# Cross-attention tile stage: whole-array products replaced by 32-row products, four tiles at a time

## The chip, the cores and the metric

The kernel runs on one core of one Trainium2 chip. The metric is the device time of one execution in microseconds (us). A profiled execution also has a span, the time from its first to its last recorded instruction, and the rows of the profile are read against that span.

## The reference

The reference is one layer of cross-attention in fp32. A text `x` of shape (4, 2048, 512) attends to a context of shape (4, 77, 384).

```python
text_p  = x @ W_text + b_text                      # 512 -> 512
audio_p = ctx @ W_audio + b_audio                  # 384 -> 512
Q = layer_norm(text_p, g1, beta1)
K = layer_norm(audio_p, g2, beta2);  V = audio_p
alpha = softmax(Q @ K.T / sqrt(512))               # over 77 keys
H = (alpha @ V) @ W_out + b_out
return layer_norm(H + x, g_out, beta_out)
```

Both kernels rearrange this. `W_text` is centred over its output channels, so that the mean of the layer norm falls away. The scores of a row are then `x` times a matrix M (512 x 77, one for each batch element), scaled by the row's reciprocal standard deviation. The variance of a row is the quadratic form x G x with G = W W^T, plus a linear term (one more column of M) and a constant. As G is symmetric, a triangle of it is enough: blocks off the diagonal are doubled, blocks above it are left out. V and `W_out` are multiplied once for each batch element, so that a row's output is its 77 softmax weights times a 77 x 512 matrix, plus `x`, normalized.

## The kernel before

The rows of `x` are worked on in 64 tiles of 128 rows; four tiles are a group, four groups a batch element. For each tile TensorE needs `x` turned (channels on partitions). That is done by VectorE's 32 x 32 block transpose, `turn` (L403), on a copy of `x` that the DMA has spread so that the blocks land in place (`spread_x`, L177, runs of 512 bytes); a second copy in natural order, `load_x` (L165), serves the residual and the quadratic form.

The tile stage, tile by tile:

- `project_chunks` multiplies the turned tile by `mu`, which holds M and the triangle of G side by side. It takes four chunks of 128 channels, each against 464, 464, 336 and 208 columns (L452), into one PSUM bank `y`, and the last 128 x 128 block of G into a second bank `yl` (L460).
- `score` (L498, L476) adds the score offsets and sums y times x, which gives the row's variance; `score_last` (L476) does the same for `yl`.
- `row_scale` (L506, L212) makes the reciprocal standard deviation on GpSimd; `scale_scores` (L513, L516), `exponential` (L523) and `invert` (L549) make the softmax weights, four tiles at a time.
- `turn_weights` transposes the weights on TensorE (L535) and copies them out on ScalarE (L536); `apply` multiplies them by the 77 x 512 matrix (L543).
- `residual` (L556) adds `x`, `squares` (L564) sums the squares, `deviations` (L576, L212) makes the reciprocal deviation. Three of four tiles are normalized on ScalarE (`norm_on_scalar`, L609) and GpSimd (`norm_on_gpsimd`, L613 and L614), the fourth by two VectorE passes (`norm_on_vector`, L593 and L595). `store` (L583) sends 128 rows to DRAM.

Ahead of the tile stage stands a preparation of some 37 us: keys and values (L246 to L309), the turned `W_text` (L634), G in `gram` (L645) and `gram_out` (L658 to L660), M in `score_weights` (L340 to L351). `value_weights` (L382) runs on TensorE between the first three tiles.

Each engine executes its instructions in the order in which the program issues them (`in_program_order`). That order is written out: a loop over the first 40 tiles and then a list of letters and tile numbers, `p` for the first half of `project_chunks`, `P` for its second half, `a` for `apply`, and so on. All DMAs are issued from the queue of SyncE (SP). PSUM has eight banks: two `y`, two `yl`, two `h`, and two for other things; `bank` hands them out. The last tiles go through softmax in twos and then one by one (`LAST`).

Of the kernel before, what the change touches and what calls it, by code (L numbers as in the profile page):

```python
# [48 lines left out]
def tile_xattn(  # L49
# [30 lines left out]
    xio = ctx.enter_context(tc.tile_pool(name="xio", bufs=5))  # L80
    xqs = ctx.enter_context(tc.tile_pool(name="xqs", bufs=2))
    scrap = ctx.enter_context(tc.tile_pool(name="scrap", bufs=1))
    soft = ctx.enter_context(tc.tile_pool(name="soft", bufs=4))
    work = ctx.enter_context(tc.tile_pool(name="work", bufs=3))
    zs = ctx.enter_context(tc.tile_pool(name="zs", bufs=13))
    small = ctx.enter_context(tc.tile_pool(name="small", bufs=8))
    ps1 = ctx.enter_context(tc.tile_pool(name="ps1", bufs=1, space=bass.MemoryType.PSUM))
    ps2 = ctx.enter_context(tc.tile_pool(name="ps2", bufs=2, space=bass.MemoryType.PSUM))

    def bank(tag, name):  # L90
        return (ps2 if tag in ("h", "y") else ps1).tile([P, 4, P], F32, tag=tag, name=name)

# [11 lines left out]
    SQ = -(-(S + 1) // Q)  # L104
    S1 = Q * SQ
    LAST_K = ND - 1
    AQ = SQ + LAST_K * R
    assert Q == ND and Q * AQ <= 4 * P

# [19 lines left out]
    wa = const.tile([P, NA, H], F32, name="wa")  # L129
# [12 lines left out]
    wc = xqs.tile([P, ND, T, P], F32, tag="xq", name="wc").rearrange("p k t c -> p k (t c)")  # L142
# [13 lines left out]
    rows = load("rows", [P, H], b_text.partition_broadcast(P))  # L156

    groups = [(b, g) for b in range(B) for g in range(NG)]
    xs, xq = {}, {}

    def load_x(i):
        if i < len(groups):
            b, g = groups[i]
            t = xio.tile([P, T, D], F32, tag="x", name=f"x_{i}")
            nc.sync.dma_start(  # L165
                out=t,
                in_=x[b, g * T * P : (g + 1) * T * P, :].rearrange("(t p) d -> p t d", p=P),
            )
            xs[i] = t

    def spread_x(i):
        if i < len(groups):
            b, g = groups[i]
            t = xqs.tile([P, T, Q, P], F32, tag="xq", name=f"xq_{i}")
            rows = x[b, g * T * P : (g + 1) * T * P, :].rearrange("(a j) c -> j a c", j=R)
            for q in range(Q):
                nc.sync.dma_start(  # L177
                    out=t[q * R : (q + 1) * R].rearrange("j t a c -> j (t a) c"),
                    in_=rows[:, :, q * P : (q + 1) * P],
                )  # L180
            xq[i] = t

    spread_x(0)
    wo = load("wo", [P, NH, H], w_out.rearrange("(k p) h -> p k h", p=P))
    bo = load("bo", [P, H], b_out.partition_broadcast(P))
    load_x(0)
    load_x(1)
    go = load("go", [P, H], g_out.partition_broadcast(P))
    beo = load("beo", [P, H], beta_out.partition_broadcast(P))
    spread_x(1)  # L190
# [23 lines left out]
    wct = const.tile([P, NH, D], F32, name="wct")  # L214
# [6 lines left out]
    mu = [const.tile([P, ND, Q, AQ], F32, name=f"mu_{i}") for i in range(2)]  # L221
    ub = const.tile([P, Q, R], F32, name="ub")

    def parts(t):
        return t.rearrange("p (q m) -> p q m", q=Q)

    made = {}
# [3 lines left out]
    va, kn, mvs, krs, vws = {}, {}, {}, {}, {}  # L231
    sizes = [z - a for a, z in key_blocks]
    columns = [slice(a, z) for a, z in key_blocks]
    cat = prep.tile([P, NA, N], F32, name="cat")
    vat = prep.tile([P, NH, N], F32, name="vat")
    kt = prep.tile([P, NH, N], F32, name="kt")
    kg = prep.tile([P, NH, B, S1], F32, name="kg")
    later = prep.tile([P, ND, B - 2, S1], F32, name="later")
# [33 lines left out]
    def values_out(j, pv):  # L272
        ba = bav[:, j : j + 1]
        if j % 2:
            nc.scalar.activation(vat[:, j], pv, AF.Identity, bias=ba)
        else:
            nc.vector.tensor_scalar(vat[:, j], pv, ba, None, ALU.add)
# [18 lines left out]

    def normed(i):

        n = sizes[i]
        kn[i] = prep.tile([P, H], F32, name=f"kn_{i}")[:n]  # L300
        nc.vector.tensor_scalar(
            kn[i], va[i], mvs[i][:n, 0:1], krs[i][:n], ALU.subtract, ALU.mult
        )
# [28 lines left out]
    def score_bank(k, tag):  # L332
        pms[k] = flat(bank(tag, f"m_ps_{k}"))[:, : B * S1].rearrange("p (b s) -> p b s", s=S1)
        nc.vector.memset(pms[k][:, :, S + 1 :], 0.0)

    def score_weights(k):

        pm = pms[k]
        for j in range(NH):
            nc.tensor.matmul(  # L340
                pm[:, :, : S + 1],
                lhsT=wct[:, j, k * P : (k + 1) * P],
                rhs=kg[:, j, :, : S + 1],
                start=(j == 0),
                stop=(j == NH - 1),
            )
        for b in range(2):
            (nc.vector.tensor_copy if b else nc.scalar.copy)(
                mu[b][:, k, :, :SQ], parts(pm[:, b, :])
            )  # L350
        nc.scalar.copy(later[:, k], pm[:, 2:, :])  # L351

    def score_offsets():
# [7 lines left out]
        for v in range(2):  # L361
            for h in range(2):
                (nc.vector.tensor_copy if h else nc.scalar.copy)(
                    uws[h * HP : (h + 1) * HP, :, v, :S],
                    pu[v * HP : (v + 1) * HP].rearrange("p (b s) -> p b s", s=S),
                )
        nc.vector.memset(uws[:, :, 0, S:], 0.0)
        nc.vector.tensor_scalar_add(bc2, bc2, H * EPS)

    vw = [  # L370
        batch.tile([P if b < 2 else S, H], F32, name=f"vw_{b}") for b in range(B)
    ]
    for b in range(B):
        made[b] = mu[b % 2], uws[:, b], vw[b][:S]

    def value_weights():

        for i, n in enumerate(sizes):
            vws[i] = (vw[i] if i < 2 else prep.tile([P, H], F32, name=f"vws_{i}"))[:n]
            pv = flat(bank("prep", f"vw_ps_{i}"))[:n]  # L380
            for j in range(NH):
                nc.tensor.matmul(  # L382
                    pv, lhsT=vat[:, j, columns[i]], rhs=wo[:, j, :], start=(j == 0), stop=(j == NH - 1)
                )
            yield
            nc.vector.tensor_tensor(vws[i], pv, bo[:n], ALU.add)
        for b in range(2, B):
            for i, (r0, r1) in enumerate(key_blocks):
                a, z = max(b * S, r0), min((b + 1) * S, r1)
                if a < z:  # L390
                    nc.sync.dma_start(
                        out=vw[b][a - b * S : z - b * S], in_=vws[i][a - r0 : z - r0]
                    )

    NT = len(groups) * T
    turned = {}

    def turn(n):

        i, t = divmod(n, T)  # L400
        if n < NT:
            xt = work.tile([P, ND, P], F32, name=f"xt_{n}", tag="xt")
            nc.vector.transpose(  # L403
                xt.rearrange("p k (a j) -> p a k j", j=R),
                xq[i][:, t].rearrange("p a (k i) -> p a k i", i=R),
            )
            turned[n] = xt


    LAST = [2, 2, 2, 2, 2, 2, 2, 1, 1]  # L410
    batches, start = [], 0
    for size in [T] * ((NT - sum(LAST)) // T) + LAST:
        batches.append(range(start, start + size))
        start += size
    batch_of = {n: tiles for tiles in batches for n in tiles}

    ys, state, kept, scored_y, in_bank = {}, {}, [], [], {}
    begun = [-1]

    class Batch:  # L420


        def __init__(self, tiles):
            f, self.tiles, self.m = tiles[0], tiles, len(tiles)
            self.uw, self.vw = made[groups[f // T][0]][1:]
            self.w = kept[0][:, groups[f // T][0], :S] if kept else self.uw[:, 1, :S]
            self.e = soft.tile([P, T, S1], F32, name=f"e_{f}", tag="e")

            def columns(name):
                return small.tile([P, T], F32, name=f"{name}_{f}", tag=name)  # L430

            self.ss, self.rs = map(columns, ("ss", "rs"))
            self.mx, self.inv = map(columns, ("mx", "inv"))
            self.sz, self.sq, self.ro, self.nm = map(columns, ("sz", "sq", "ro", "nm"))
            self.z = {}

    def of(n):

        tiles = batch_of[n]
        f = tiles[0]  # L440
        if f not in state:
            state[f] = Batch(tiles)
        return state[f], slice(n - f, n - f + 1)


    def project_chunks(n, ks):
        mub = made[groups[n // T][0]][0]
        xt = turned[n]
        y, b = ys[n]
        for k in ks:  # L450
            cols = slice(0, SQ + min(k + 1, LAST_K) * R)
            nc.tensor.matmul(  # L452
                parts(y[:, : Q * AQ])[:, :, cols],
                lhsT=xt[:, k, :],
                rhs=mub[:, k, :, cols],
                start=(k == LAST_K),
                stop=(k == 0),
            )
            if k == LAST_K:
                nc.tensor.matmul(  # L460
# [429 lines left out]
```

## Time and profile before

| | |
|---|---|
| median of 3 runs | 293.08 us (293.02 to 293.49) |
| span of the profiled execution | 291.9 us |
| TensorE busy | 283.0 us (97%) |
| VectorE busy | 227.1 us (78%) |
| GpSimd busy | 157.2 us (54%) |
| ScalarE busy | 153.3 us (53%) |
| DMA packets | 54178, 55.33 MB |
| first tile product (L452) starts | 37.21 us |

The profile came without a device time of its own for the profiled execution; its span is 1.2 us under the median of the runs. A row of a group reads: line, engine, operation, output tile from input tiles, shape, count, then busy us and the mean ns of one, then the idle time of the engine ahead of it and what ended that idle time. A row of the timeline starts with the time in us from the start of the span and the length. The ends of matmuls are modelled, so their spacing is read from their starts.

### The profile page before, as it was taken

What the parts mean: (1) busy time and instruction counts of PE and PEld (TensorE: products, weight loads), DVE (VectorE), ACT (ScalarE), POOL (GpSimd) and SP (SyncE); (2) the same over time, 40 slices, a digit from 0 to 9 for tenths busy, and PEclk for the clock granted to TensorE, in tenths of its full rate; (3) what the DMA queues carried; (4) which work ended last, traced back from release to release, by engine and by line L of the source; (5) the groups of instructions that cost most, each with busy time, mean ns of one, the idle gap of its engine ahead of it and who ended that gap; (6) DMA issues with size and microseconds to landing.
All of it is one profiled execution on the core that took longest, in us unless ns stands there. A gap on an engine that the chain in (4) does not pass through costs nothing.

```text
span 291.9 us, 4021 instructions
## 1 busy us (share of the span) xinstructions
PE 283.0 (97%) x1034; PEld 171.6 (59%) x1034; DVE 227.1 (78%) x715; ACT 153.3 (53%) x486; POOL 157.2 (54%) x168
## 2 busy tenths in 40 slices
PE   8999999999999999999999999999999999999990
PEld 7786755565555555555555555556555556555540
DVE  1586133586878888888888989898999999989995
ACT  2646210031446383838383838366967767477571
POOL 1022000011026576757676767687989878977833
PEclk9999999999999999999999999999999999999996
DMA  6899913359390967887777878789689887612214
GB/s 200 212 267 370 214 65 99 61 183 249 92 227 36 186 245 161 274 171 263 167 265 165 269 162 270 160 274 206 262 174 294 200 270 204 159 72 88 108 58 180
DMA packets 54178, 55.33 MB, mean 190 GB/s; under 512 B 2597, under 2 KB 35697, under 8 KB 54155
## 3 DMA queue, kind: packets, MB, share of 16 engines
q1 hardware_dynamic: 54155, 55.07, 70.0%
q8 instruction: 8, 0.13, 0.2%
q14 instruction: 15, 0.12, 0.2%
HBM read 37.97 MB, written 16.78 MB: 188 GB/s over the span
## 4 chain that ended last, share of the span: by engine, by line
PE 94%; DVE 3%; issue 1%; DVEq 0%; ACT 0%
PE y L452 53%; PE h L543 18%; PE yl L460 5%; PE vw_ps L382 4%; PE m_ps L340 3%; PE vat_ps L264 3%; PE et_ps L535 2%; PE w_ps_yl L645 2%; PE w_ps_yl L208 1%; PE w_ps_y L645 1%; DVE z L595 1%; PE uw_ps L358 1%; DVE z L556 1%; DVE y L593 1%; PE va_ps L284 0%
## 5 line engine op out<-in xcount | busy, mean ns | idle before, releaser
L452 PE MATMUL y<-mu,xt 128*128 128x464 f32 (+2 forms) x512 | 179.6, 473 | 0.0
L452 PEld LDWEIGHTS y<-mu,xt 128*128 128x128 f32 x512 | 89.7, 190 | 49.6 <-issue 32.3
L543 PE MATMUL h<-vw,et 77*128 77x512 f32 x128 | 64.1, 594 | 0.1
L564 ACT ACTIVATE sqj<-z,sz 128x512 f32<-128x512 f32 x64 | 46.0, 718 | 31.9 <-DVE z L556 31.0
L613 POOL TENSOR_TENSOR z<-z,go 128x512 f32<-128x512 f32 x44 | 56.0, 1272 | 10.0 <-ACT z L609 9.4
L614 POOL TENSOR_TENSOR z<-z,beo 128x512 f32<-128x512 f32 x44 | 55.9, 1271 | 3.5
L556 DVE SCALAR_TENSOR_TENSOR z<-h,inv,x 128x512 f32<-128x512 f32 x64 | 46.5, 733 | 2.3 <-PE h L543 1.7
L403 DVE STREAM_TRANSPOSE xt<-xq 128x512 f32<-128x512 f32 x64 | 44.7, 704 | 0.5 <-PE y L452 0.5
L476 DVE CUSTOM_DVE_ANT_1 yl<-yl,x,bc 128x128 f32<-128x128 f32 x64 | 22.6, 353 | 28.2 <-PE yl L460 28.1
L476 DVE CUSTOM_DVE_ANT_1 y<-y,x,e 128x384 f32<-128x384 f32 x64 | 40.1, 626 | 2.3
L506 POOL TENSOR_SCALAR rs<-ss 128x4 f32<-128x4 f32 (+2 forms) x21 | 4.7, 223 | 66.9 <-DVE ss L476 66.6
L460 PEld LDWEIGHTS yl<-ub,xt 128*128 128x128 f32 x128 | 23.6, 188 | 26.2 <-issue 15.6
L609 ACT ACTIVATE z<-z,no,ro 128x512 f32<-128x512 f32 x44 | 34.5, 802 | 0.1
L536 ACT COPY et<-et_ps 77x256 f32<-77x256 f32 (+1 forms) x33 | 11.9, 361 | 39.5 <-PE et_ps L535 39.5
L212 POOL TENSOR_TENSOR ro<-ro,mhalf 128x4 f32<-128x4 f32 (+2 forms) x21 | 18.2, 867 | 23.7 <-ACT ro L576 23.6
L523 ACT ACTIVATE e<-e,mx 128x77 f32<-128x77 f32 x64 | 22.2, 349 | 11.9 <-DVE mx L516 11.9
L543 PEld LDWEIGHTS h<-vw,et 77*128 77x128 f32 x128 | 23.3, 190 | 7.0 <-issue 5.2
L460 PE MATMUL yl<-ub,xt 128*128 128x128 f32 x128 | 24.5, 273 | 0.0
L212 POOL TENSOR_TENSOR rs<-rs,mhalf 128x4 f32<-128x4 f32 (+2 forms) x21 | 18.6, 886 | 1.8
L498 DVE TENSOR_TENSOR e<-y,uws 128x80 f32<-128x80 f32 x64 | 15.0, 234 | 4.6 <-PE y L452 3.4
L535 PEld LDWEIGHTS et_ps<-ident,e 128*77 128x77 f32 x64 | 9.4, 147 | 15.1 <-issue 10.7
L593 DVE SCALAR_TENSOR_TENSOR y<-z,nm,gain_ps 128x512 f32<-128x512 f32 x20 | 14.9, 752 | 0.8
(107 smaller groups left out, 254.5 us busy)
## 6 DMA issues: line engine op xcount, KB each, us to landing
xq<-in_x_dram SPq DMA_DIRECT2D x64, 256.0 KB, 4.9
x<-in_x_dram SPq DMA_DIRECT2D x16, 1024.0 KB, 6.1
out_dram<-z SPq DMA_DIRECT2D x64, 256.0 KB, 2.5
wc<-in_L_xattn_W_text_dram SPq DMA_DIRECT2D x4, 256.0 KB, 5.2
wo<-in_L_xattn_W_out_dram SPq DMA_DIRECT2D x1, 1024.0 KB
wa<-in_L_xattn_W_audio_dram SPq DMA_DIRECT2D x3, 256.0 KB, 3.6
rows<-in_L_xattn_b_text_dram SPq DMA_DIRECT2D x1, 256.0 KB
bo<-in_L_xattn_b_out_dram SPq DMA_DIRECT2D x1, 256.0 KB
```

The costliest lines, as they stand in the source:

```text
L212: nc.gpsimd.tensor_tensor(dst, v, mhalf[: v.shape[0], : v.shape[1]], ALU.pow)
L403: nc.vector.transpose(xt.rearrange("p k (a j) -> p a k j", j=R), xq[i][:, t].rearrange("p a (k i) -> p a k i", i=R),)
L452: nc.tensor.matmul(parts(y[:, : Q * AQ])[:, :, cols], lhsT=xt[:, k, :], rhs=mub[:, k, :, cols], start=(k == LAST_K), stop=(k == 0),)
L460: nc.tensor.matmul(b, lhsT=xt[:, k, :], rhs=ub.rearrange("p q i -> p (q i)"), start=True, stop=True)
L476: nc.vector.tensor_tensor_reduce(out=y, in0=y, in1=x, scale=1.0, scalar=first, op0=ALU.mult, op1=ALU.add, accum_out=to)
L523: nc.scalar.activation(e, e, AF.Exp, bias=s.mx[:, c], accum_out=s.inv[:, c])
L543: nc.tensor.matmul(s.h[n], lhsT=s.et[:, n - s.tiles[0], :], rhs=s.vw, start=True, stop=True)
L556: nc.vector.scalar_tensor_tensor(z, s.h.pop(n), s.inv[:, c], xs[i][:, t, :], ALU.mult, ALU.add, accum_out=s.sz[:, c])
L564: nc.scalar.activation(junk, s.z[n], AF.Square, bias=s.sz[:, c], scale=-float(H), accum_out=s.sq[:, c])
L609: nc.scalar.activation(z, z, AF.Identity, bias=s.no[:, c], scale=s.ro[:, c])
L613: nc.gpsimd.tensor_tensor(z, z, go, ALU.mult)
L614: nc.gpsimd.tensor_tensor(z, z, beo, ALU.add)
```

## The change

The tile stage is rewritten. TensorE is used as four row groups of 32 rows: group g works on tile g of a group of four (now called a quad), with 32 channels of `x` on its 32 partitions. The four tiles of a quad are loaded so that a 32 x 32 block transpose alone puts tile a on partitions 32a to 32a+31, all 16 chunks of 32 channels side by side in `xt`.

- G's triangle is kept in blocks of 32 channels, so each tile takes 16 products for the main bank (`Y`, 110 to 494 columns), 3 for a side bank (`L`, 96, 64 and 32 columns) and 3 for the output (`H`, 512 columns, the 77 keys in pieces of 32). Each row group has two PSUM banks: `a0` to `a3` for `Y`, `b0` to `b3` for `L` and `H` in turn.
- The right-hand sides lie on every group of 32 partitions: `spread_gram` copies G there in 64 small DMAs, `spread_scores_first` copies M of the first batch element in 16, followed by 16 copies on three engines (`place_scores_first`). A second buffer `gq_1` is filled by one DMA during quad 1 (`second_gram`); M of each later batch element is written by 64 small DMAs (`spread_scores`).
- The softmax weights are scaled by the reciprocal sum on ScalarE (`weights`) and turned by one VectorE block transpose for four tiles (`turn_weights`); the transposes on TensorE and their copies on ScalarE are gone. The scaling of the scores moves from VectorE to ScalarE (`scale_scores`).
- Normalization is on ScalarE and GpSimd for every tile of the first 13 quads (`norm_on_scalar`, `gain_on_gpsimd`, `shift_on_gpsimd`); the VectorE version serves some tiles of the last three.
- `x` in natural order is loaded in rows of 2 KB, the copy to be turned in runs of 8 KB; the residual and the output are made in place in the latter.
- The order of TensorE's products comes from `passes` and `queue`: each group has its own list, group g starts `SKEW` times g later, and the lists are merged by planned start. The other steps are a new written list, with `pN` for "issue products up to number N".

```diff
+    def turn(n, a):
+        if a == 0:
+            turned[n] = work.tile([P, NC, P], F32, name=f"xt_{n}", tag="xt")
+        nc.vector.transpose(
+            turned[n][:, :, a * R : (a + 1) * R],
+            xq[n][:, a, :].rearrange("p (k i) -> p k i", i=R),
+        )
+    def passes():
+        for n in range(NQ):
+            for at, k in enumerate(reversed(range(NC))):
+                if at == LPOS:
+                    for last in reversed(range(NM, NC)):
+                        yield "L", n, last, (last + 1 - NM) * R
+                yield "Y", n, k, U + min((k + 1) * R, MAIN)
+            if n:
+                for p in range(NP):
+                    yield "H", n - 1, p, H
...
+    queue = []
+    for g in range(Q):
+        at = g * SKEW
+        for kind, n, k, cols in passes():
+            queue.append((at, g, kind, n, k))
+            at += max(cols, P + 2)
+    queue.sort(key=lambda e: e[:2])
...
+        if kind == "Y":
+            if g == 0 and k in (NC - 1, NC // 2):
+                transfers(n, k < NC - 1)
+            if k == NC - 1:
+                main[n, g] = flat(bank(f"a{g}", f"y_{n}_{g}"))
+            m = U + min((k + 1) * R, MAIN)
+            nc.tensor.matmul(
+                main[n, g][:, :m],
+                lhsT=turned[n][group, k, :],
+                rhs=gq[b % 2][group, OFF[k] : OFF[k] + m],
+                start=(k == NC - 1),
+                stop=(k == 0),
+            )
...
+    def turn_weights(n):
+        s = state[n]
+        nc.vector.transpose(
+            s.et.rearrange("q p t j -> q t p j"), s.en.rearrange("q t (p i) -> q t p i", i=R)
+        )
...
+    def spread_gram(K):
+        for q in range(Q):
+            k = K * Q + q
+            for g in range(Q):
+                nc.sync.dma_start(
+                    out=gq[0][g * R : (g + 1) * R, OFF[k] + U : OFF[k] + WIDE[k]],
+                    in_=gn[q * R : (q + 1) * R, K, : (k + 1) * R],
+                )
+    def spread_scores_first():
+        for q in range(Q):
+            for g in range(Q):
+                nc.sync.dma_start(
+                    out=sr[g * R : (g + 1) * R, q], in_=ms[q * R : (q + 1) * R, :, 0, :U]
+                )
+    def second_gram():
+        gq.append(batch.tile([P, GW], F32, tag="gq_1", name="gq_1"))
+        nc.sync.dma_start(out=gq[1], in_=gq[0])
+    def transfers(n, late):
+        b, g = divmod(n, NG)
+        if not late:
+            load_x(n + 1)
+        else:
+            spread_x(n + 2)
+            if n == 1:
+                second_gram()
+            if n in (0, 1):
+                spread_values(n + 2)
+        if b == 0 and g >= 2:
+            spread_scores(1, 2 * g - 4 + late)
+        elif 1 <= b < B - 1 and not late:
+            spread_scores(b + 1, g)
```

## Prediction

> **What bounds the kernel now.** I read the page's busy shares first, then the chain that ended last, then the rate of the tiles in that chain, then the timeline for prices.
>
> ```profile
> PE 283.0 (97%) x1034; PEld 171.6 (59%) x1034; DVE 227.1 (78%) x715; ACT 153.3 (53%) x486; POOL 157.2 (54%) x168
> ...
> PEclk9999999999999999999999999999999999999996
> ...
> PE 94%; DVE 3%; issue 1%; DVEq 0%; ACT 0%
> ```
>
> TensorE holds 94% of the last chain, and the clock row shows it at full clock until the last slice. Only fewer or overlapping products can shorten the middle of the run. The tile rate stands in the chain in order of time, four tiles between two like rows:
>
> ```profile
> 94.42 1.70 PE y L452 x6
> ...
> 109.10 1.70 PE y L452 x6
> ```
>
> That is 14.68 us for four tiles. The price of a product comes from the starts in the timeline:
>
> ```profile
> 151.97 0.94 PE L452 MATMUL y<-mu,xt 128*128 128x464 f32 x2
> ...
> 152.75 0.38 PE L460 MATMUL yl<-ub,xt 128*128 128x128 f32 x2
> ...
> 152.97 1.86 PE L452 MATMUL y<-mu,xt 128*128 128x464 f32 x6
> ...
> 154.67 1.02 PE L543 MATMUL h<-vw,et 77*128 77x512 f32 x2
> ...
> 155.53 0.38 PE L535 MATMUL et_ps<-ident,e 128*77 128x128 f32 x2
> ...
> 155.75 0.55 PE L452 MATMUL y<-mu,xt 128*128 128x464 f32 x1
> ```
>
> Each fp32 product is two MATMULs (x2), each with its own weight load. 464 columns take 0.78 us and 512 take 0.86: 1.68 ns per column. 128 columns take 0.22 us, so a pass and its load cost 0.11 us. Four tiles are 4 x (1472 + 128 + 512) = 8448 columns, 14.2 us, plus four transposes at 0.11: 14.6, as the chain has it. TensorE never waits.
>
> The last two views are for what joins TensorE as a limit: the DMA issues, and the groups of GpSimd.
>
> ```profile
> 7.50 0.25 SPq L152 DMA_DIRECT2D vec_rows<-in_L_xattn_beta_dram  x1
> ...
> 9.67 0.25 SPq L152 DMA_DIRECT2D vec_rows<-in_L_xattn_beta_dram  x1
> 9.96 0.35 SPq L113 DMA_DIRECT2D rows<-in_L_xattn_b_text_dram  x1
> ```
> ```profile
> L613 POOL TENSOR_TENSOR z<-z,go 128x512 f32<-128x512 f32 x44 | 56.0, 1272 | 10.0 <-ACT z L609 9.4
> L614 POOL TENSOR_TENSOR z<-z,beo 128x512 f32<-128x512 f32 x44 | 55.9, 1271 | 3.5
> ```
>
> A small DMA holds SP for 0.29 us (9.67 to 9.96), a larger one for 0.40 (9.96 to the next at 10.36). The gain and the shift cost GpSimd 2.54 us per tile.
>
> **The change part by part**, against the span of 291.9; the median is 1.2 above it.
>
> 1. *Products.* Per tile, Y has 16 products of 78 columns plus 32 to 416: 5408. L has 192 and H 1536. A product under 130 columns is bounded by its two loads (0.22 us), so L counts 390 and Y 5428: 7354 in all. If the four row groups really stream at once, each at 1.68 ns per column, a quad takes 7354 x 1.68 = 12.35 us, against 14.68. Sixteen quads save 37.3. No row of this trace has two products in flight, so this rate is assumed, not read; the rivals price what happens without it. Loads of a group stay hidden if they run beside other groups' passes, as they run beside their own group's now. TensorE gets 88 x 2 pairs of load and pass per quad, one per 0.070 us. The four transposes of `kt_ps` from 19.59 to 19.86 went at 0.067, so the issue of instructions just reaches.
>
> 2. *Start of the stage.* It now waits for DMAs. G's first block is copied by VectorE behind `kn`, which ended at 21.40 in the trace, so the issues begin at about 21.7. 64 DMAs of G and 16 of M follow on SP: at 0.29 to 0.38 each (0.38 is the 0.33 of a store plus its gap) 23.2 to 30.4 us. Landing of the last takes about 2 us (a store lands in 2.5 on the page), and its copy 0.2. The first product starts between 47.1 and 54.5; I take 51, the middle. Before, the stage began at 37.21, with 10.3 us of `vw_ps` (3 x 3.44, from 39.90 to 43.34) between its tiles, which now runs in the wait: 47.5 in like terms. Cost 3.5 (-0.4 to 7).
>
> 3. *Change of batch.* In the middle of quad 1, at about 66 us, a copy of 128 x 5600 fp32 (2.87 MB) is issued. At the 387 GB/s of the stretch from 20 to 26 us it takes 7.4 us, at the steady 222 GB/s 12.9. The 64 DMAs of M for batch 1 follow it, with some 16 loads among them. All sit on SP in order: 80 x 0.29 to 0.38 is 23 to 30 us. The blocks that quad 4 reads first are issued last. They land between 99 and 113, while quad 4 is due at 51 + 9.8 + 3 x 12.35 = 98. Stall 1 to 15; I take 8. The later batches issue 25 DMAs per quad, 7.3 to 9.5 us of SP in 12.35: taken 2 (0 to 5). A store that waits for GpSimd holds SP, and with it the load of the quad after next; that is what the 2 is for.
>
> 4. *VectorE per quad*, by spacing in the trace: turn 4 x 0.63, side sums 4 x 0.24 (0.27 less 32 elements), scores 4 x 0.27, main sums 4 x 0.57, residual 4 x 0.64, weights turned 0.50, shift 0.4, maximum 0.42, small ones 0.5: 11.2 us. It no longer scales scores, and `norm_on_vector` is gone. Under 12.35: nothing.
>
> 5. *ScalarE per quad*: squares 4 x 0.71, normalization 4 x 0.71, exponentials 4 x 0.34, scores and weights 8 x 0.25, variances 0.2: 9.2 us. Nothing.
>
> 6. *GpSimd per quad*: 4 x 2.54 plus two reciprocal roots at 1.04 and 1.02 (the L212 groups): 12.2 us. It is level with TensorE. The softmax's root queues behind the gains of the quad before. Cost 2 (0 to 8): it shifts output, and only late buffers would push back.
>
> 7. *Tail.* The last quad has four tiles in softmax at once, not one. From its last Y product: scores and sums 4 x 0.85, clamp 0.3, root 1.04, scales 1.0, shift and maximum 0.8, exponentials 1.4, reciprocal 0.1, weights 1.0, turn 0.5, ten handovers near 0.09: 10.5 us. Then H 2.6 with the last group 0.9 behind, residual 0.6, squares 0.9, variance and root 1.0, four tiles' worth of VectorE passes (4 x 1.4), store and end 3.5: 15.1. Y of quad 15 ends at 51 + 16 x 9.77 + 14 x 2.58 = 243.4 in the sum's own time, so the end is 243.4 + 25.6 = 269, which is 20.4 beyond 51 + 16 x 12.35. Before: 37.21 + 10.3 + 16 x 14.68 = 282.4, 9.5 short of the end. Cost 10.9 (8 to 15).
>
> Sum: 291.9 - 37.3 + 3.5 + 10 + 2 + 10.9 = 281.0, as a median 282.2. The likeliest case gives **282** us. Its own range takes the low ends of items 2, 3, 6 and 7 (3.9 + 9 + 2 + 2.9, together 17.8) and their high ends (3.5 + 10 + 6 + 4.1, together 23.6): 264 to 306.
>
> *A rule weighed against this.* The Trainium skill, "TensorE: Matmul & The Clock Gate", Part 3, says that matmuls in different row groups run beside each other, and gives 3.07x for four of them at 512 columns. By 3.07 in place of 4 a quad would be 16.1 us and the sum an estimated 342. The same part says that MATMULs start strictly in program order; that rule speaks for the second rival below. No row of this trace shows either.
>
> **Rivals.**
>
> *Loads one at a time (slower).* The place is TensorE's weight path. A quad has 176 loads; the trace's 128-column row prices a load with its pass at 0.11, so a quad takes 19.4 us. 16 x (19.4 - 12.35) is +113; the stalls of items 3 and 6 (12) hide in it: about 383 as a median. It decides from the load at which the sum is 291.9: 10.9 spare over 16 quads is 0.68 us, 13.03 per quad, 0.074 us per load. For it: no two loads of fp32 products start less than 0.11 apart in the rows above. Against: those all go to the whole array, and the loads of different groups fill different cells.
>
> *Two in flight, not four (the change doesn't do what it says).* A product's two passes stand next to each other in TensorE's queue (x2 in every row). If passes start in program order, the second waits for the first and holds back the other groups, so only two streams overlap. A quad takes half of 4 x 7354 x 1.68 = 49.4, that is 24.7 us: 16 x 12.35 = +198, 12 of it hiding stalls, 468 as a median. For it: every pass in the trace starts when the one before has streamed. Against: before, all passes need all rows, so they could not do otherwise. If loads too kept to the order, a load of 0.11 would add to each of 88 passes of 0.28 in a row: 34 us per quad, over 600.
>
> *DMAs bound the stage.* Four streams work, but SP or the copies hold longer than I took: 0.38 per issue, quad 4 at 113, later batches 5, GpSimd 8. That is 3.5 + 10 + 6 over the sum, 302. [...]
>
> **How the numbers follow.** The likeliest case, four streams, has 0.62: below 292.5 in 0.43, within 0.2% (about what a measurement of this kernel can tell from no change) in 0.03, and above in 0.16, where the DMA rival lies. Loads one at a time 0.13, two in flight 0.17, strict order 0.04, something between 0.04. So faster 0.43, same 0.03, slower 0.54: the likeliest single case is faster, while the slower cases together hold more. The forecast time is that case's 282. To leave out no more than 2 in 10 the range has to reach over the loads' 383 to the two streams' 468: 264 to 472.
>
> **What would show it.** Right: products (L474 in the changed kernel) of four row groups starting less than 0.1 us apart on average, Y of successive quads 12.3 to 13 us apart, first product near 51, one wait of TensorE on a DMA of `gq` ahead of quad 4, TensorE idle about 10 us before the last H. Wrong by the rivals: quads 19 us apart with loads back to back, or 25 us apart with second passes waiting. A VectorE or GpSimd operation that runs longer beside four streams than in the rows above would spoil items 4 and 6.

## The result, and the profile after

The changed kernel takes 419.06 us as the median of four runs (418.80 to 420.51), against 293.09 (293.02 to 293.49): 1.430 times as long, with a 95% interval of 1.427 to 1.433. The forecast was 282; the time lies inside the range given, on its slow side. The profiled execution spans 416.9 us, 125.0 more than before.

The page of the changed kernel, with the lines that answer to those shown of before: busy shares, clock by slices of 10.4 us, DMA share by slices, and the chain that ended last by engine and by line.

```profile
PE 292.7 (70%) x3009; PEld 253.0 (61%) x3009; DVE 218.7 (52%) x701; ACT 170.3 (41%) x510; POOL 179.3 (43%) x174
...
PEclk9989965595899765599696966996979679999755
DMA  6701233999992353446564748483738389962214
...
DMA 42%; PE 23%; SPq 21%; DVE 7%; ACT 3%; issue 3%; POOL 0%; DVEq 0%
DMA x<-in_x_dram 18%; DMA xq<-in_x_dram 14%; SPq L693 13%; PE y L474 8%; DMA vwq<-vwa 5%; DMA gq<-gq 5%; PE h L497 4%; PE m_ps L363 2%; PE vw_ps L407 2%; SPq L679 2%; SPq L670 2%; PE vat_ps L284 2%; SPq L198 1%; SPq L421 1%; DVE xq L662 1%
```

TensorE held 94% of the chain before and holds 23% now. DMAs and their issues on SP hold 63%. The clock falls in the slices where TensorE waits.

SP's timeline at the start (start, duration, line, transfer, number):

```profile
20.90 40.86 SPq L670 DMA_DIRECT2D gq<-gn  x64
61.88 10.35 SPq L679 DMA_DIRECT2D sr<-ms  x16
```

The 64 DMAs of G hold SP for 40.86 us without a gap, 0.64 each, and the 16 of M for 0.65 each. The first product is at 77.5 us, where 51 was forecast.

SP's timeline over one quad in the middle:

```profile
190.20 0.58 SPq L204 DMA_DIRECT2D xq<-in_x_dram  x1
190.88 2.54 SPq L641 DMA_DIRECT2D out_dram<-xq  x4
193.51 3.71 SPq L198 DMA_DIRECT2D x<-in_x_dram  x4
197.99 12.19 SPq L693 DMA_DIRECT2D gq<-ms  x16
210.22 0.58 SPq L204 DMA_DIRECT2D xq<-in_x_dram  x1
```

From one load of `xq` to the next, SP always has a next DMA that it is issuing or waiting to issue, and that takes 20.0 us. This is about the period of the stage. The chain of the same stretch holds no TensorE at all: 6.70 us for `xq` to land, 7.67 for x, then nine issues of 0.59 (start, us, what; the issues between are left out).

```profile
190.20 6.70 DMA xq<-in_x_dram
...
196.91 7.67 DMA x<-in_x_dram
...
204.60 0.51 SPq L693
...
209.59 0.59 SPq L693
...
210.22 6.37 DMA xq<-in_x_dram
```

The list of SP's waits from 182.9 to 346.3 us (quads 4 to 12; total, number, longest of each) shows that not all of SP's time is issuing:

```profile
SPq L693 <- DMA x<-in_x_dram: 16.5, 25, 0.8
SPq L693 <- DMA out_dram<-xq: 8.3, 13, 1.7
SPq L198 <- DMA xq<-in_x_dram: 7.5, 8, 1.4
SPq L641 <- POOL xq L653: 2.7, 8, 0.6
```

A small DMA of M needs neither x nor a store. In the trace every DMA signals the same semaphore as the eighth one before it (101 and 103 to 109, in turn), and it waits on that semaphore first. So a DMA is issued only when the eighth before it has landed. Of these 163.4 us SP issued for some 117 and, by the whole list, waited 35.0 for that eighth landing and 2.9 for other things. The chain above is this window at work: the last of the four loads of x stands eight places behind `xq`, a DMA of M eight places behind that one, and nine issues later the next `xq` comes. That is 8 + 8 + 9 = 25 DMAs, one quad's.

To compare runs, most of them a single execution each, I take the time from one quad to the next, by VectorE's first `s<-y` of each quad:

| run | first product | quads 2 to 4 | quads 4 to 12, each | last four, each | time |
|---|---|---|---|---|---|
| changed kernel | 77.5 | 57.4 | 20.4 | 13.0 | 419.1 |
| later M left out | 77.4 | 32.2 | 13.1 | 13.1 | 335.8 |
| and copy left out | 77.8 | 26.9 | 13.2 | 13.1 | 333.1 |
| and main sums light | 77.6 | 25.8 | 12.9 | 12.9 | 326.6 |
| M and G by way of DRAM | 80.3 | 41.9 | 13.1 | 13.1 | 348.9 |
| two queues | 68.9 | 43.5 | 18.7 | 13.0 | 396.8 |
| M from DRAM, same shape | 77.9 | 52.9 | 18.5 | 13.1 | 401.8 |
| tiny loads | 77.6 | 38.0 | 18.2 | 13.5 | 385.4 |
| lower bound | 57.2 | 26.9 | 13.2 | 13.1 | 308.9 |
| lower bound, light | 57.2 | 25.8 | 12.9 | 12.9 | 297.2 |

### The profile page after: what moved, and what is told of

Read it like the earlier page. It is cut to its first block, busy times and chain, and to the rows that moved or that the text cites. A ratio compares the mean times of both kernels' runs of the same rounds, so it can differ in the third digit from the quotient of the medians.

```text
span 416.9 us, 8278 instructions
## 1 busy us (share of the span) xinstructions
PE 292.7 (70%) x3009; PEld 253.0 (61%) x3009; DVE 218.7 (52%) x701; ACT 170.3 (41%) x510; POOL 179.3 (43%) x174
## 2 busy tenths in 40 slices
DMA packets 38799, 66.11 MB, mean 159 GB/s; under 512 B 15770, under 2 KB 17638, under 8 KB 36582
## 4 chain that ended last, share of the span: by engine, by line
DMA 42%; PE 23%; SPq 21%; DVE 7%; ACT 3%; issue 3%; POOL 0%; DVEq 0%
DMA x<-in_x_dram 18%; DMA xq<-in_x_dram 14%; SPq L693 13%; PE y L474 8%; DMA vwq<-vwa 5%; DMA gq<-gq 5%; PE h L497 4%; PE m_ps L363 2%; PE vw_ps L407 2%; SPq L679 2%; SPq L670 2%; PE vat_ps L284 2%; SPq L198 1%; SPq L421 1%; DVE xq L662 1%
## 5 line engine op out<-in xcount | busy, mean ns | idle before, releaser
L474 PE MATMUL y<-gq,xt 32*128 32x494 f32 (+12 forms) x2048 | 201.1, 485 | 56.2 <-DVE xt L431 26.6
L474 PEld LDWEIGHTS y<-gq,xt 32*128 32x128 f32 x2048 | 182.2, 200 | 72.2 <-issue 39.9
L497 PE MATMUL h<-vwq,et 32*128 32x512 f32 (+1 forms) x384 | 83.5, 779 | 52.6 <-DVE s L541 34.4
L649 POOL TENSOR_TENSOR xq<-xq,go 128x512 f32<-128x512 f32 x56 | 69.9, 1270 | 76.0 <-ACT xq L645 76.0
L497 PEld LDWEIGHTS h<-vwq,et 32*128 32x128 f32 (+1 forms) x384 | 58.9, 252 | 59.9 <-issue 47.8
L610 ACT ACTIVATE sqj<-xq,sz 128x512 f32<-128x512 f32 x64 | 46.0, 718 | 78.0 <-DVE xq L602 77.0
L653 POOL TENSOR_TENSOR xq<-xq,beo 128x512 f32<-128x512 f32 x56 | 70.7, 1284 | 0.2
L602 DVE SCALAR_TENSOR_TENSOR xq<-h,xq 128x512 f32<-128x512 f32 x64 | 40.9, 686 | 31.0 <-PE h L497 30.7
L645 ACT ACTIVATE xq<-xq,no,ro 128x512 f32<-128x512 f32 x56 | 41.1, 801 | 9.5 <-DVE no L635 9.3
L531 DVE CUSTOM_DVE_ANT_0 y<-y,x,sl 128x416 f32<-128x416 f32 x64 | 40.6, 654 | 0.7
L231 POOL TENSOR_TENSOR ss<-ss,mhalf 128x4 f32<-128x4 f32 x16 | 16.2, 1011 | 53.0 <-DVE ss L554 52.9
## 6 DMA issues: line engine op xcount, KB each, us to landing
vwq<-vwa SPq DMA_DIRECT2D x16, 192.0 KB, 11.2
gq<-gq SPq DMA_DIRECT2D x1, 2800.0 KB, 19.3
```

The lines of the kernel that those rows point to most:

```text
L231: nc.gpsimd.tensor_tensor(dst, v, mhalf[: v.shape[0], : v.shape[1]], ALU.pow)
L474: nc.tensor.matmul(main[n, g][:, :m], lhsT=turned[n][group, k, :], rhs=gq[b % 2][group, OFF[k] : OFF[k] + m], start=(k == NC - 1), stop=(k ...
L497: nc.tensor.matmul(s.h[g], lhsT=s.et[rows, k].rearrange("p t j -> p (t j)"), rhs=vwq[b][rows, k, :], start=(k == 0), stop=(k == NP - 1),)
L531: nc.vector.tensor_tensor_reduce(out=y, in0=y, in1=x, scale=1.0, scalar=first, op0=ALU.mult, op1=ALU.add, accum_out=to)
L602: nc.vector.scalar_tensor_tensor(z, s.h.pop(a), 1.0, z, ALU.mult, ALU.add, accum_out=s.sz[:, a : a + 1])
L610: nc.scalar.activation(junk, z_of(n, a), AF.Square, bias=s.sz[:, c], scale=-float(H), accum_out=s.sq[:, c])
```

## Experiments

My first theory was that the issues of the small DMAs on SP hold the stage. The rivals were that TensorE does not sustain four streams, and that landings or packets are slow whatever the number of issues.

### The later batches' M left out

```
-        if b == 0 and g >= 2:
-            spread_scores(1, 2 * g - 4 + late)
-        elif 1 <= b < B - 1 and not late:
-            spread_scores(b + 1, g)
```

> Left out: the 64 small DMAs per batch that put the score columns M of batches 1 to 3 into `gq`, so that all batches use the M of batch 0 (the output is that of another function). Theory (the DMA issues on SP hold the stage: 16 of them per quad at 0.63 us are 10 us of SP): quads 4 to 11 go from about 20.3 us to 12.4 to 14 us each, as quads 12 to 15 do already, and quads 2 to 4 lose the wait for M but keep that for the copy of `gq`; about 419 - 8 x 7.6 - 24 = 334 us. Rival A (TensorE does not sustain four streams; the last quads are special): quads stay near 20 us, over 390 us. Rival B (loads land late because their landing, not their issue, is slow): 16 to 18 us per quad, about 360 to 380 us.

Measured 335.79, and 13.1 us per quad. The 192 DMAs cost 83.3 us: 58 in quads 4 to 12 and 25 between quads 2 and 4. TensorE sustains its streams in the middle as well as at the end.

### The copy of `gq` left out too

```
-            if n == 1:
-                second_gram()
...
-                rhs=gq[b % 2][...]
+                rhs=gq[0][...]
```

> As the run without the score columns of batches 1 to 3, and besides without the copy of `gq` to its second buffer: all batches read one buffer. Theory: quads 1 to 4 now also run at 12.4 to 14 us, and about 8 to 15 us go from the time with M left out alone: near 322 us. Rival (the copy is hidden, x and xq alone set these quads): the same time as with M left out alone, within 3 us.

Measured 333.06. The copy lands 19.3 us after its issue in the changed kernel, yet it costs 2.7 us in the end, with the later M left out; with M in place its cost was not measured. Quads 2 to 4 gain 5.4 us; the quads before came 1.9 us later in this run, and the one after takes 0.7 longer. The rival was right here. The windows of this run show what a steady quad is made of (window, its length, then busy us and count for TensorE, its loads, VectorE, ScalarE and GpSimd; granted clock; DMA share; GB/s):

```profile
207.00:291.00 84.00, 81.72 (x1106) 79.10 (x1108) 77.21 (x254) 61.22 (x178) 77.26 (x65) 1.00 0.77 227
250.00:263.00 13.00, 12.89 (x180) 12.42 (x176) 11.78 (x40) 9.74 (x29) 12.26 (x11) 1.00 0.83 244
```

TensorE is busy 97% of the time at full clock. In 13.0 us it takes 176 loads, one per 0.074 us. Its timeline shows the streams side by side:

```profile
254.97 1.42 PE L474 MATMUL y<-gq,xt 32*128 32x430 f32 x12
```

The row is named after its first pass; its twelve passes have 430, 398 or 366 columns, 4776 in all. One after another they would take 4776 x 0.84 ns = 4.0 us at the price of before. The thirteenth pass starts 1.03 us after the first (256.00 against 254.97). Their starts, taken one by one from the trace, fall into four rows, each spaced by its own columns at that price:

| row | starts in us (columns) |
|---|---|
| 1 | 254.971 (430), 255.331 (398), 255.668 (398), 256.001 (366) |
| 2 | 255.109 (398), 255.446 (398), 255.779 (366) |
| 3 | 255.116 (398), 255.449 (366), 255.756 (366) |
| 4 | 255.182 (430), 255.542 (430), 255.902 (398) |

Between the two passes of 398 columns in row 2 a pass of each other row starts.

### G and M by way of DRAM, in a quarter of the DMAs

```
-            for g in range(Q):
-                nc.sync.dma_start(
-                    out=gq[b % 2][g * R : (g + 1) * R, OFF[k] : OFF[k] + U],
-                    in_=ms[q * R : (q + 1) * R, K, b, :U],
-                )
+            nc.sync.dma_start(
+                out=gq[b % 2][:, OFF[k] : OFF[k] + U],
+                in_=four_times(md[q * R : (q + 1) * R, K, b]),
+            )
```

`md` is a copy of `ms` in DRAM, and `four_times` repeats its 32 rows for the four groups. G goes the same way.

> The whole computation. The blocks of G and M are first written to DRAM, and each DMA then fills all four row groups (128 partitions) from there: 16 DMAs of G in place of 64, 4 in place of 16 for the first M, 16 in place of 64 for each later M; five more DMAs write to DRAM. Packets and bytes into `gq` are the same. Theory (the number of issues on SP counts; one of 128 partitions takes about 0.45 us): the first product comes near 52 us in place of 77.5, quads 4 to 11 take 12.4 to 14.5 us; about 419 - 26 - 8 x 7 - 20 = 317 us. Rival (the packets and their landing count, not the issues): first product after 70 us, quads near 20 us, over 390 us.

Measured 348.85: right for the stage, wrong for the start. Quads 4 to 12 take 13.1 us with the same bytes into `gq` and nearly as many packets in the whole run (37358 against 38799), so the number of DMAs counts there. SP's timeline has slack again (nothing between 212.00 and 213.64, for instance):

```profile
209.05 2.95 SPq L642 DMA_DIRECT2D out_dram<-xq  x4
213.64 2.08 SPq L199 DMA_DIRECT2D x<-in_x_dram  x4
215.82 3.47 SPq L699 DMA_DIRECT2D gq<-md  x4
219.41 3.29 SPq L205 DMA_DIRECT2D xq<-in_x_dram  x1
```

The start did not move, because the way through DRAM has landings of its own. The chain of this run holds them (start, us, transfer):

```profile
30.11 6.05 DMA gd<-gn
38.50 8.96 DMA gd<-gn
49.14 0.66 SPq L677
49.91 13.15 DMA md<-ms
```

### Half of the small DMAs from ScalarE's queue

```
-                nc.sync.dma_start(
+                (nc.scalar if g % 2 else nc.sync).dma_start(
```

> The whole computation: of every four small DMAs that fill the row groups of G and M, two are issued from ScalarE's queue and two from SP's. Theory (each queue issues one of these per 0.63 us, and two queues issue side by side): the first product comes 40 x 0.63 = 25 us earlier than 77.5, but not before the last M is there, so near 56; in quads 4 to 11 SP has 17 issues (about 9.5 us) and ScalarE 8 x 0.6 on top of 10.5 us of work, 15.3 us, so quads of about 15.5 us; about 419 - 21 - 8 x 5 - 20 = 338 us. Rival (the queues share what makes a descriptor, or the packets are the limit): first product after 70 us and quads near 20 us, over 390 us.

Measured 396.76. At the start the two queues do issue side by side, each at 0.67 us per DMA or less: ScalarE's 8 DMAs from 21.55 take 5.37 us while SP's run. (SP's 27.34 us below include waits between the four blocks of G.)

```profile
21.54 27.34 SPq L670 DMA_DIRECT2D gq<-gn  x32
50.50 5.18 SPq L679 DMA_DIRECT2D sr<-ms  x8
```

The first product comes 8.6 us earlier, not 21, since ScalarE scales the keys only after its DMAs, and the products of M start at 38.5 us (28.3 in the lower bound below). In the stage, quads take 18.7 us with half the issues on each queue. My theory does not explain that. In quads 4 to 12 SP waited 63.0 us for landings, 44.0 of it for DMAs of M, for which it had not waited before: the window of eight is shared by both queues. For instance, a DMA of M on ScalarE's queue starts at 237.89, when the load of `xq` that SP issued at 231.49 with the same semaphore has landed (237.87). The other way round, SP's load of x at 258.32 follows the landing (258.26) of a DMA of M that ScalarE issued at 251.75. ScalarE's own work also stands behind the waits of its DMAs, and single quads take 13.3 to 27.4 us. So the issue time alone is not the limit.

The Trainium skill, "DMA: Bandwidth & Descriptors", section "Issuing engines are not separate DMA queues", says that issuing from several engines saves only the sequencer's time, which is usually small beside the DMA. The first half agrees with 22 us gained of 126. The second does not describe these DMAs: the issue holds SP for 0.59 us of the 2.1 until they land, and 80 of them make up most of the wait at the start.

### As many DMAs, but cheap ones

```
-                    out=gq[b % 2][g * R : (g + 1) * R, OFF[k] : OFF[k] + U],
-                    in_=ms[q * R : (q + 1) * R, K, b, :U],
+                nc.sync.dma_start(out=tiny[:, count[0]], in_=rows_of(x, 0)[:4, :8])
```

> Each of the 192 DMAs that bring M of batches 1 to 3 is replaced, in its place in SP's order, by a load of 4 x 8 numbers from DRAM that nobody reads (left out: the later batches' M). The number of DMAs stays, as does the rule that a DMA waits for the landing of the eighth before it; the time of one issue falls from 0.59 to about 0.25 us. Theory (issue time on SP): 9 x 0.5 + 16 x 0.29 = 9.1 us per quad, so quads 4 to 11 at 13.1 to 14 us and about 336 to 345 us. Rival (the number of DMAs in order and the landings they wait for, which two queues did not cure either): quads of 16 to 19 us, 365 to 390 us.

Measured 385.42 and 18.2 us per quad, by the rival. One issue took 0.29 us (median), and SP's issuing in quads 4 to 12 fell from some 117 to 79 us. Its waits for the eighth landing grew from 35.0 to 57.1. Issue time that is saved turns into waiting, as the list of SP's waits shows:

```profile
SPq L696 <- DMA x<-in_x_dram: 30.0, 32, 2.4
SPq L696 <- DMA out_dram<-xq: 15.6, 28, 1.8
SPq L198 <- DMA xq<-in_x_dram: 8.0, 8, 1.8
```

The chain of a quad has the same three links as in the changed kernel, with the same count of nine issues between the last two lines:

```profile
231.15 6.21 DMA xq<-in_x_dram
...
237.37 7.71 DMA x<-in_x_dram
...
245.10 0.25 SPq L696
...
248.10 6.22 DMA xq<-in_x_dram
```

That is 16.95 us in place of 20.02: the landings stay, and only the nine issues got shorter. So the stage is bound by 25 DMAs per quad in one order with eight under way, nine of which are large and land in 7 to 8 us. With 13 per quad the limit is gone. Why a load of x takes 8.1 us to land in the changed kernel, and 5.6 with the later M left out, was not tried.

### As many DMAs of the same shape, from DRAM

```
-                    in_=ms[q * R : (q + 1) * R, K, b, :U],
+                    in_=rows_of(x, b)[g * R : (g + 1) * R, :U],
```

> The 192 DMAs of M for batches 1 to 3 keep their place, their number, their destination and their size (32 rows of 312 bytes), but read rows of x in DRAM in place of M in SBUF (so the later batches' scores are others). Issue time: if the SBUF source is what made it 0.59 us, it falls to 0.31 to 0.36 as for the x loads; if the 32 short rows do, it stays at 0.59. Theory (16 more DMAs in one order, each waiting for the landing of the eighth before it): with 0.33 per issue quads 4 to 11 take 17 to 18.5 us as with the tiny loads, 380 to 395 us; with 0.59 they stay at 20 and the time at 410 to 419.

Measured 401.81. One issue took 0.42 us against 0.59, between the two cases, so both the source in SBUF and the rows (32 of 312 bytes, against 4 of 32) have a part in the price. Quads take 18.5 us, close to the tiny loads' 18.2, as the theory of the window has it. The total is above what it gave, 380 to 395: quads 2 to 4 take 52.9 us against 38.0, since here quad 4 does wait for what is loaded (TensorE's longest wait for a DMA into `gq` is 13.8 us; the tiny loads have none).

### The replication left out: a lower bound

```
-            for g in range(Q):
-                nc.sync.dma_start(
-                    out=gq[0][g * R : (g + 1) * R, OFF[k] + U : OFF[k] + WIDE[k]],
-                    in_=gn[q * R : (q + 1) * R, K, : (k + 1) * R],
-                )
+            nc.sync.dma_start(
+                out=gq[0][:, OFF[k] + U : OFF[k] + WIDE[k]], in_=gn[:, K, : (k + 1) * R]
+            )
```

> A lower bound. Left out, on top of the later batches' M and the copy of `gq`: the replication. Each block of G goes to `gq` in one DMA from 128 rows to the same 128 rows, the first M in four, so each row group multiplies other rows of G than it should; 20 DMAs in place of 80. The first two x tiles are loaded early, ahead of them. Theory (the 80 issues hold the start): first product near 55 us, no wait of quad 1 for x; 333 - 23 - 6 = about 304 us, still above the 293 before, because a quad takes 13.1 us and the last 30 us have one quad in them. Rival (the start waits for the landing of M or for vector work, not for the issues): first product after 70 us, about 325 us.

x of the first two quads is loaded ahead of these DMAs (not shown above), and M of the first batch goes in 4 DMAs. Measured 308.94, with the first product at 57.2. So some 20 us of the late start are the DMAs of the replication. The chain of this run, around the start, shows what holds the rest:

```profile
40.70 10.31 PE vw_ps L409 x24
51.03 0.69 DVE vwa L418
51.72 2.40 DVE xt L433 x4
54.12 0.63 DVE gq L683 x6
54.75 2.41 DVE xt L433 x4
57.20 9.98 PE y L476 x70
```

`vw_ps` no longer runs in a wait. It stands ahead of the first product, with VectorE's bias, turns and copies behind it.

### TensorE kept warm

```
+    keep_warm(112)
     for a in range(Q):
         turn(0, a)
```

> The whole computation, with 112 products of zeros on TensorE between the last product of the preparation (51 us) and the first of the tile stage (77.5 us), so that its clock does not fall in that wait. Theory (the clock of TensorE is a consequence, the DMAs set the pace): quad 0's products take about 8 us in place of 10 to 14, but quad 1 still waits for x and vwq; 0 to 3 us less than 419. Rival (the halved clock is what makes the early quads slow): quads 0 and 1 at 12.4 to 13 us, 8 to 12 us less.

Measured 419.42: no gain. The clock was 1.00 from 52 to 78 us, and the quads came as before. The half clock is a consequence of the stalls there, not their cause.

For the wait ahead of the last H, the products of zeros go into a bank that VectorE's passes give up:

```
+    def warm_again(*_):
+        t = flat(bank("a0", "again_ps"))
+        for _ in range(33):
+            nc.tensor.matmul(t[:, :P], lhsT=zeros, rhs=zeros, start=True, stop=True)
...
-        y = flat(bank(f"a{a % 3}", f"no_ps_{n}_{a}"))
+        y = flat(bank(f"a{1 + a % 2}", f"no_ps_{n}_{a}"))
```

> The whole computation, with 33 products of zeros on TensorE between the last Y and the last quad's H, in a PSUM bank that two of VectorE's passes give up. Theory (the clock that fell to half in the last softmax makes the last H take 8.4 us in place of about 4): 3 to 5 us less than 419. Rival (what follows H is paced by VectorE and GpSimd anyway): 0 to 1 us less.

Measured 418.03. The last H, in the chain of the changed kernel and then of this run:

```profile
396.68 8.38 PE h L497 x26
```

```profile
398.75 3.98 PE h L497 x24
```

H is 4.4 us shorter at full clock (1.00 over it, against 0.50 in the changed kernel), and from the last Y to the end it is 28.1 us in place of 30.7. The total shows less, since the last Y came 2.1 us later in this run.

### VectorE's main sum cut

```
-        y = main.pop((n, t))[:, U : U + MAIN]
+        y = main.pop((n, t))[:, U : U + R]
```

> Against the time with the later batches' M and the copy of `gq` left out (333.1). Left out besides: 384 of the 416 columns of each tile's main sum, so VectorE has about 1.6 us less to do per quad. Theory (the steady 13.1 us of a quad are TensorE's own four streams, 6% off the ideal 12.35): quads stay at 13.0 to 13.2 us, under 2 us less in all but for the first quads. Rival (VectorE's handovers hold the steady quads): quads at 12.4 to 12.6 us, 8 to 10 us less.

Measured 326.61, and 12.9 us per quad against 13.2: between the two. Some 0.3 us per quad were VectorE's main sum. Over quads 5 to 11 the chain now holds 71% TensorE, with 13% VectorE and 12% ScalarE; with the full sums it held 47%, 25% and 23%. So it is not shown that what is left above 12.35 us is TensorE's own.

### The bound made lighter

```
+    keep_warm(18)
     for a in range(Q):
         turn(0, a)
...
-        y = main.pop((n, t))[:, U : U + MAIN]
+        y = main.pop((n, t))[:, U : U + R]
```

The products of zeros ahead of the last H are in it too.

> The lower bound (308.9: no replication, no later M, no copy of `gq`, x early) made lighter still: main sums of 32 columns in place of 416 (left out: the rest of the sum), and products of zeros that keep TensorE's clock up ahead of the first product and ahead of the last H. Theory (four streams at 12.85 us per quad, a start at 57 and a tail of 28): 308.9 - 16 x 0.25 - 2.6 - 1 to 4 = 298 to 301 us, still slower than before. Rival (the stage's stalls and the clock cost more than that): under 293, in which case a version of the change that beats the kernel before would be within reach.

Measured 297.15 (294.72 to 297.85): 1.011 times the kernel before, 95% interval 1.006 to 1.017. Even without the replication, the later M, the copy and most of VectorE's main sum, and with a warm clock, the four streams do not beat it. No run here points to a whole version that would.

## Why the prediction was wrong

The step that failed is what the small DMAs cost. The working had them at 0.29 to 0.38 us of SP each, where they took 0.63, and it put no limit on how many are under way, where there were eight. Item 3 put 10 us on the change of batch and the later batches; leaving out those DMAs and the copy gave back 86.0. Item 2 put 3.5 us on the late start; the first product came 30.0 us later in like terms.

The times lead down a ladder: 419.1 as changed; 83.3 less without the later M; 2.7 less without the copy; 24.1 less without the replication at the start and with x early; 11.8 less with light sums and a warm clock. That is 297.2, and 4.1 more than before is left.

*Item 1, the products, held in mechanism.* Four row groups stream at once, and neither "loads one at a time" nor "two in flight" happened: loads start as little as 0.007 us apart (255.111 and 255.118 in the run without the copy, each 0.18 long), and the second pass of a product does not hold back the other groups. Four full streams are 49.4 us of passes per quad (short products at the forecast's 130 columns), so 13.1 is 3.8 at once; the forecast's 12.35 was 4. The gain is 16 x (14.68 - 13.1) = 25.3 us, not 37.3. The text gave 13.03 us per quad as the point where nothing is left of the gain. The steady rate is beyond it, before any stall. Of the 0.75 us above 12.35, 0.3 were VectorE's main sum; where the rest goes is open. The rule of the Trainium skill, "TensorE: Matmul & The Clock Gate", Part 3, section "Measured speedup vs the span model", 3.07 times for four, would have put a quad at an estimated 16.1 us; the trace decides for 13.1.

*Item 2, the start, failed at the price of an issue.* (The upper end of its own sum is 54.3, not 54.5; nothing hangs on it.) The forecast took 0.29 to 0.38 us from loads out of DRAM to four rows and from stores. These DMAs go from SBUF to SBUF and cost 0.63 from start to start. The trace of before had rows nearer in kind, and I passed them over (SP's timeline of before):

```profile
51.66 0.79 SPq L391 DMA_DIRECT2D vw<-vw  x1
57.79 1.62 SPq L391 DMA_DIRECT2D vw<-vws  x2
```

At 0.79 each, 80 of them are 63 us, and the first product would have been put beyond 85; it came at 77.5. The lower bound adds that 6 us of the miss are not the replication's: "which now runs in the wait" was wrong for `vw_ps`, since the turned x and the placed M come behind it.

*Item 3, the later batches, turned the sign.* "25 DMAs per quad, 7.3 to 9.5 us of SP in 12.35: taken 2" should have been about 20 us per quad. They cost 7.3 us in each of eight quads, 58 us in all, and 25 more between quads 2 and 4, where a stall of 8 was forecast for M and the copy together. Two things are in it: the price of an issue, and the window of eight DMAs, which the working did not have. The trace of before has the same order of semaphores in all its DMAs, but there it cost next to nothing: by the list of SP's waits, under 5 us in the whole run. Of the 7.3 us, 2.2 went when only the issues were made cheap, while all went when there were 12 fewer DMAs per quad. For the copy, 7.4 to 12.9 us were forecast and it landed in 19.3, at little cost.

*Items 4 to 6.* The forecast had 11.2, 9.2 and 12.2 us per quad for VectorE, ScalarE and GpSimd. The steady window has 11.78, 9.74 and 12.26. VectorE was not quite free: 0.3 us per quad. The 2 us for GpSimd do not show once the DMAs are gone.

*Item 7, the tail.* The last softmax took 10.5 us from the last Y to H (386.2 to 396.7), as forecast. H took 8.4 in place of 3.5, because TensorE had waited and its clock was at half. In all 30.7 us in place of 25.6.

The sum's first quads also had a cost that no item named. In the lower bound quad 0 to 1 takes 20.6 us, with the products of each group starting behind that group's main sum (2.01 us of products, then 0.66 of VectorE, in turn). There is no H of an earlier quad to fill in. That cause is read from the chain and was not tried by itself; in the light lower bound, where the main sum takes 0.26, the quad takes 19.5.

The rival "DMAs bound the stage" named the right place and was priced at 302, because it took 0.38 per issue and 5 us for all later batches. The range held the time by the reach that the other rivals gave it, and that is luck: the two rivals that held 0.30 of the 0.54 for "slower" did not happen, and the likeliest case was the right mechanism with the wrong price of its DMAs.

## What to carry to other kernels

Count the DMAs of a steady period before the bytes: multiply them by the issue price of the row of the same kind (same source, same number of rows), and then ask how many may be under way and which large one stands eight places ahead. Work that must be replicated to row groups belongs in few DMAs, or in none. When a change trades TensorE time for waits, price the later work at the clock that it will then have.

## What was not expected of the hardware

One issue on SP took 0.59 us for 32 rows from SBUF to SBUF, 0.42 for the same rows from DRAM, and 0.29 for four short rows from DRAM. Two queues issue side by side without slowing each other at the start: 0.59 us on SP (median) while ScalarE's took 0.60. Products of fp32 in four row groups reach 3.8 streams over a steady quad, although each is two passes. The wait of some eight microseconds ahead of the last H was enough to halve TensorE's clock, and took H from 4.0 us to 8.4.
